# A list scheduler with fifteen fixed shifts of rank, and a third engine for one multiplication

## The chip, the cores and the metric

One NeuronCore of a Trainium2 chip. The metric is the device time of one execution in microseconds, the median of several runs of the same program.

The engines that matter here: TensorE (PE: matrix products, with PEld for its weight loads), VectorE (DVE), ScalarE (ACT), GpSimd (POOL), and SyncE (SP), which in this kernel issues nearly all DMA transfers, in order. Each engine runs its own queue in order and waits on semaphores for the others. The matrix products write to PSUM, in eight banks.

## What is computed

One post-layernorm transformer block in fp32 on x of shape (2, 512, 512), cut here to what matters:

```python
# attention: 32 query heads, 8 key/value heads (groups of 4), head width 128
q, k, v = heads(x @ Wq.T), heads(x @ Wk.T), heads(x @ Wv.T)
q, k = rmsnorm(q, q_norm_w), rmsnorm(k, k_norm_w)   # t * rsqrt(mean(t*t) + eps) * w
s = q k^T / sqrt(128) + where(rel > 0, -1e30, slope[h] * rel)
x = layernorm(x + (softmax(s) v) @ Wo.T)
# feed-forward, int32 weights with a scale per output
h = silu(gate(x)) * up(x)                           # 512 -> 1376
x = layernorm(x + down(h))                          # 1376 -> 512
```

## The kernel before, in words

**Tiles and stages.** The 1024 tokens are 8 tiles of 128 rows. Attention runs in *units*: one key/value head group g (8 of them), one batch entry b (2), one tile i of 128 queries (4), so 64 units. Two neighbouring units are a *pair* (32 pairs): its projection of 768 columns (4 query heads, one key head, one value head, each 128 wide) is made together.

For a pair, `project` (L816; the first pair has `project_plain`, L778) multiplies x by the group's weights with a scheme of seven products on half blocks (`seven`, matmuls on L674), whose sums and differences of operands (`sums_a`, `sums_b`, all recorded on L615) are made by VectorE or GpSimd. ScalarE or VectorE evicts the banks to the tile c (L771, L773), and VectorE adds others to it (L615).

`heads` (L909) then normalises the five normed heads (four query, one key) of each of the pair's two row tiles r. ScalarE squares 640 columns of c into sq (L924). VectorE sums each head to ms (L933). An epsilon is added (L947), and GpSimd raises ms to -1/2, which gives inv (L601). Then, for each r, one `tensor_tensor` multiplies c by inv, broadcast over each head's 128 columns, into sq; VectorE or GpSimd does it (L615, tiles sq<-c,inv). VectorE turns sq in blocks into c (L1069); this goes to HBM and back in another order (far_q<-c L1082, qT<-far_q L1093), and ScalarE or GpSimd weighs the key head into kT (L1107). Two (g, b) of the sixteen take their transposes from TensorE (L1026, L1041) and not from HBM.

`scores` (L1127) makes, per unit, four matmuls sc (L1144; each leaves two records in the trace), adds the bias and takes the row maxima on VectorE (L1153), the exponential on ScalarE (L1169) and the division by the row sum on ScalarE or GpSimd (L1201, L1203). `attend` (L1215) turns the attention weights: VectorE in blocks (st, L891), out to HBM (far<-st, L900) and back (prT<-far, L1264); TensorE multiplies them by v (pa, L1287; px and pz, L1319). The results aT are multiplied by Wo in an inner and outer scheme (L1511, or L674 for the last two groups) and added to acc. After the last group come layernorm (`norm1`, transposes on L1660), the feed-forward products (tiles p..._h and p..._d on L674) and the last layernorm.

**What sets the order.** Nothing is emitted when the Python code runs through these functions. `Work.add` only records an operation: a price per engine that may do it, a rank (`prio`), the function that emits it, and what it reads and writes. `Work.emit` is a greedy list scheduler: it keeps an own clock for every engine and for the DMA transfers, asks for every ready operation and every engine that may do it when it could start (inputs ready, engine free, a buffer free in the ring), and emits on each step the one that starts first; at equal starts the lower rank goes first, then the one that ends first. The instruction order of every queue, the engine of each flexible operation and the buffer of each tile come out of this.

The prices are simple lines: `pe(n) = max(0.14, n / 600)`, `act(n) = 0.15 + 0.00084 n` (0.1 more with a scale per row), `dve(n) = 0.15 + 0.00106 n`, `pool_tt(n) = 0.27 + 0.00197 n`. A transfer of m MB takes m / 0.3 us of one shared DMA clock, starts 1.6 us after its issue at the earliest, and ends 0.6 us after its share; an issue holds SP for 0.6 us. Operations marked `port` on VectorE and all of GpSimd's exclude each other in the plan.

**Ranks.** A unit u has ranks near u: its scores u, `attend` u + 0.4; a pair's projection u - 2.4 and its `heads` u - 1.8 to u - 1.4; Wqkv of a new group is loaded at u - 14, Wo at u - 10, and multiplied out near u + 2.6. The feed-forward ranks begin at 67. The start (first weights, x, the masks) has ranks from -9 to -1.

Of the kernel before, what the change touches and what calls it, by code (L numbers as in the profile page):

```python
# [2 lines left out]

# [9 lines left out]
AF = mybir.ActivationFunctionType  # L13
ALU = mybir.AluOpType
AX = mybir.AxisListType
ENG = mybir.EngineType

P = 128
B, S, DM = 2, 512, 512
H, HKV, HD = 32, 8, 128  # L20
G = H // HKV
# [37 lines left out]
def act(n, scaled=False):  # L59
    return 0.15 + 0.00084 * n + (0.1 if scaled else 0.0)  # L60


def dve(n):
    return 0.15 + 0.00106 * n


def pool_tt(n):
    return 0.27 + 0.00197 * n
# [5 lines left out]

LAG = {"PE": 0.22, "DVE": 0.1, "ACT": 0.12, "POOL": 0.2, "SP": 0.1, "ACTQ": 0.1, "NONE": 0.0}
TABLE = 1.28


class Ring:


    def __init__(self, name, bufs, shape, dtype=F32):
        self.name, self.bufs, self.shape, self.dtype = name, bufs, shape, dtype
        self.pool = None
        self.slots = [None] * bufs
        self.later = None

    def add(self, ring):

# [2 lines left out]
    def room(self, but=()):  # L92

        best = None
        if self.pool is not None:
            for k, b in enumerate(self.slots):
                if (self, k) in but:
                    continue
                t = 0.0
                for u in b.users if b else ():  # L100
                    if u["end"] is None:
                        break
                    t = max(t, u["end"] + LAG[u["eng"]])
                else:
                    if best is None or t < best[0]:
                        best = (t, self, k)
        if self.later is not None:
            found = self.later.room(but)
            if found is not None and (best is None or found[0] < best[0]):
                best = found  # L110
        return best

    def take(self, b):
        _, ring, k = self.room()
        ring.slots[k] = b
        b.tile = ring.pool.tile(
            ring.shape, ring.dtype, tag=f"{ring.name}{k}", name=b.name, bufs=1
        )


class Buf:


    def __init__(self, ring, name):
        self.ring, self.name = ring, name
        self.users = []
        self.tile = None

    def __getitem__(self, i):
        return self.tile[i]  # L130
# [2 lines left out]
class Work:  # L133


    def __init__(self):
        self.ops = []
        self.wrote, self.read = {}, {}

    def add(  # L140
        self,
        costs,
        prio,
        fn,
        reads=(),
        writes=(),
        after=(),
        table=None,
        lag=0.0,
        port=False,  # L150
        issue=0.6,
    ):


        op = {
            "issue": issue,
            "costs": costs,
            "prio": prio,
            "fn": fn,
            "deps": set(id(o) for o in after),  # L160
            "obj": list(after),
            "takes": [],
            "end": None,
            "table": table,
            "lag": lag,
            "port": port,
            "n": len(self.ops),
        }
        deps = {id(o): o for o in after}
        for key in reads:  # L170
            o = self.wrote.get(key)
            assert o is not None, (key[0].name, key[1])
            deps[id(o)] = o
        for key in writes:
            o = self.wrote.get(key)
            if o is not None:
                deps[id(o)] = o
            for o in self.read.get(key, ()):
                deps[id(o)] = o
        for key in reads:  # L180
            if key not in writes:
                self.read.setdefault(key, []).append(op)
        for key in writes:
            self.wrote[key] = op
            self.read[key] = []
        bufs = []
        for key in list(reads) + list(writes):
            b = key[0]
            if b not in bufs:
                bufs.append(b)  # L190
        for b in bufs:
            op["takes"].append(b)
            b.users.append(op)
        op["deps"] = list(deps.values())
        self.ops.append(op)
        return op

    def emit(self):
        ops = self.ops
        left = [len(o["deps"]) for o in ops]  # L200
        nexts = [[] for _ in ops]
        for o in ops:
# [6 lines left out]
        def at(o):  # L209
            t = 0.0  # L210
            for d in o["deps"]:
                t = max(t, d["end"] + d["lag"])
            return t

        for o in ops:
            if not left[o["n"]]:
                o["at"] = 0.0
                ready.append(o)
        emitted = 0
        port = {"DVE": 0.0, "POOL": 0.0}  # L220

        def room(o):

            t, but = o["at"], []
            for b in o["takes"]:
                if b.tile is not None:
                    continue
                found = b.ring.room(but)
                if found is None:
                    return None  # L230
                t = max(t, found[0])
                but.append(found[1:])
            return t

        while ready:
# [16 lines left out]
            for e, found in at_engine.items():  # L252
                first = min(found)
# [3 lines left out]
            o = ops[n]  # L257
# [14 lines left out]
                if e == "POOL" or (e == "DVE" and o["port"]):  # L272
                    port[e] = s + c
            o["start"] = s
            o["lag"] += LAG[e]
            for b in o["takes"]:
                if b.tile is None:
                    b.ring.take(b)
            o["fn"](e)
            emitted += 1  # L280
            for x in nexts[o["n"]]:
                left[x["n"]] -= 1
                if not left[x["n"]]:
                    x["at"] = at(x)
                    ready.append(x)
        assert emitted == len(ops)


@with_exitstack
def post_ln_block(  # L290
# [17 lines left out]
    nc = tc.nc  # L308
# [4 lines left out]
    W = Work()  # L313
    vec = {"DVE": nc.vector, "POOL": nc.gpsimd}
# [10 lines left out]
    rings = {}  # L325

    def ring(stage, name, bufs, shape, dtype=F32):
        r = Ring(name, bufs, shape, dtype)
        rings.setdefault(stage, []).append(r)
        return r  # L330

    def fixed(ring_, name):
# [277 lines left out]
    def tensor(n, prio, dst, a, b, alu, reads, writes, who=("DVE", "POOL"), sbuf=None, after=()):  # L610
        cost = {"DVE": dve(n), "POOL": pool_tt(n)}
        W.add(
            {e: cost[e] for e in who},
            prio,
            lambda e: vec[e].tensor_tensor(dst(), a(), b(), alu),  # L615
            reads,
            writes,
            after,
            port=len(who) > 1 if sbuf is None else sbuf,
        )  # L620
# [288 lines left out]
    def heads(p, prio):  # L909
# [7 lines left out]
        kT, v = kTs[g, b], vs[g, b]  # L917
        sq = Buf(r_sq, f"sq_{p}")
        ms, inv = Buf(r_ms, f"ms_{p}"), Buf(r_inv, f"inv_{p}")
        for r in range(2):  # L920
            W.add(
                {"ACT": act(5 * HD) + 0.05},
                prio,
                lambda e, r=r: nc.scalar.activation(  # L924
                    sq[:, r].rearrange("p h d -> p (h d)"), c(r)[:, : 5 * HD], AF.Square
                ),
                [(cb, (r, 0)), (cb, (r, 1))],
                [(sq, r)],
            )
            W.add(  # L930
                {"DVE": 0.15 + 0.135 * (G + 1)},
                prio,
                lambda e, r=r: nc.vector.tensor_reduce(ms[:, r], sq[:, r], AX.X, ALU.add),  # L933
                [(sq, r)],
                [(ms, r)],
            )


        for rs in ((0,), (1,)) if p == 0 else ((0, 1),):
# [20 lines left out]
            if p == 0:  # L960
                lead.append(W.ops[-1])
        for r in range(2):
            tensor(
                5 * HD,
                prio,
                lambda r=r: sq[:, r],
                lambda r=r: c(r)[:, : 5 * HD].rearrange("p (h d) -> p h d", h=G + 1),
                lambda r=r: inv[:, r].unsqueeze(2).to_broadcast([P, G + 1, HD]),
                ALU.mult,
                [(cb, (r, 0)), (cb, (r, 1)), (inv, r)],  # L970
                [(sq, r)],
            )


# [754 lines left out]
    def close(stage, opens, side, ends):  # L1729
        def fn(e):  # L1730
            stages[stage].close()
            for r in rings[opens]:
                r.pool = open_pool(opens, f"p_{r.name}", r.bufs, side, reuse_waits="tile")

        return W.add({"NONE": 0.0}, 0.0, fn, (), (), ends)

    def users(stage):
        seen = {}
        for o in W.ops:
            for b in o["takes"]:  # L1740
                if b.ring in rings[stage]:
                    for u in b.users:
                        seen[u["n"]] = u
        return list(seen.values())

    close("qkv", "up", "left", users("qkv"))
    close("att", "down", "right", users("att"))

    r_wi = ring("up", "wi", 1, [P, 2, NK, P], I32)
    r_wf = ring("up", "wf", 1, [P, 2, NK, P])  # L1750
# [10 lines left out]
    r_ds = ring("down", "ds", 1, [P, DM])  # L1761
    for r in (r_wi, r_wf, r_sw, r_gu):
        r.add(ring("down", r.name + "b", 1, r.shape, r.dtype))

    load(0.01, -6.0, lambda q: q.dma_start(gs_sb.tile, gs), [A(gs_sb)])
    load(0.01, -6.0, lambda q: q.dma_start(us_sb.tile, us), [A(us_sb)])
# [351 lines left out]
```

## Time and profile before

| | us |
|---|---|
| median of 3 runs | 984.5 (983.72 to 985.08) |
| the profiled execution | 983.08 |
| its span, first to last instruction | 981.3 |
| TensorE busy in it | 957.2 |
| VectorE, GpSimd, ScalarE busy | 731.4, 535.6, 451.8 |
| HBM traffic | 92.62 MB read, 53.48 MB written |

The profile is of one execution. A page sums it up: the busy time of each engine, the chain of work that ended last, the costliest groups of instructions. Groups are told apart by source line, engine, operation and the tiles they write and read (out<-in); helpers record many operations on one line, so the tiles matter more than the line. Behind a group's count stand its busy time, the mean duration of one, and the idle time of its engine just before it with what ended that. Other views give waits (who waited for whom), stretches (busy time of each engine between two times), the timeline and the chain in order of time. The clock in them is the share of TensorE's full clock that was granted. The largest single DMA groups are the attention weights' way out (112 issues of 256 KB, median 3.0 us from issue to landing) and back (224 of 128 KB, 3.1 us); a weight load of 384 KB has 5.3 us and Wo's 1024 KB 5.7 us.

### The profile page before, as it was taken

Reading aid. Unit: us, or ns where it says so; the run is one execution under the profiler, and the core shown is the slowest. Engines: PE = TensorE matmul, PEld = TensorE weight load, DVE = VectorE, ACT = ScalarE, POOL = GpSimd, SP = SyncE. Lnnn points to the kernel's source line nnn. Section 1 sums busy time; section 2 is a strip of 40 time slices with the busy share of each in tenths; the row PEclk is TensorE's granted clock in tenths of the full one; section 3 lists DMA queues with packets and bytes.
Section 4 is the critical chain, followed back from the end, with each engine's and each line's share of the span. In section 5 each row is a group of like instructions: output and inputs, shape, how many; then the busy total and the mean of one; then the engine's idle time right before and its main releaser. Section 6 shows DMA issues by size and latency. Waiting matters only on the chain.

```text
span 981.3 us, 14068 instructions
## 1 busy us (share of the span) xinstructions
PE 957.2 (98%) x4330; PEld 692.4 (71%) x4330; DVE 731.4 (75%) x1780; ACT 451.8 (46%) x1209; POOL 535.6 (55%) x582
## 2 busy tenths in 40 slices
PE   8999999999999999999999989999979999999997
PEld 5666766676767776766767666667757788888886
DVE  8777787778787788787887878797866676667544
ACT  2465364646464556456464646464445243333000
POOL 5675575868564854867386847864552322123120
PEclk9899999999999999999999999999989999999999
DMA  8123748764755765586558676656451232210001
GB/s 305 52 102 104 208 134 255 219 190 148 232 161 151 225 200 155 172 258 194 165 153 249 202 217 203 193 144 211 111 157 59 64 98 86 81 52 22 22 22 43
DMA packets 182795, 147.69 MB, mean 151 GB/s; under 512 B 26208, under 2 KB 166368, under 8 KB 181440
## 3 DMA queue, kind: packets, MB, share of 16 engines
q1 hardware_dynamic: 181856, 146.13, 48.9%
q8 instruction: 35, 0.57, 0.2%
q10 hardware_dynamic: 864, 0.66, 0.2%
q14 instruction: 40, 0.33, 0.1%
HBM read 92.62 MB, written 53.48 MB: 149 GB/s over the span
## 4 chain that ended last, share of the span: by engine, by line
PE 91%; DMA 4%; DVE 2%; SPq 1%; POOL 1%; issue 0%; ACT 0%; POOLq 0%; DVEq 0%; ACTq 0%
PE pa_q L674 15%; PE sc L1144 12%; PE pa L1287 11%; PE pa_h L674 8%; PE pb_q L674 8%; PE pa_o L1511 8%; PE pc_q L674 4%; PE pb_h L674 4%; PE pb_o L1511 4%; PE pa_d L674 4%; PE pa_o L674 3%; PE pc_o L1511 2%; DMA prT<-far 2%; PE pc_h L674 2%; PE pb_d L674 2%; PE px L1319 2%
## 5 line engine op out<-in xcount | busy, mean ns | idle before, releaser
L1169 ACT ACTIVATE pr<-pr,nmax 128x48 f32<-128x48 f32 (+15 forms) x256 | 133.5, 522 | 94.7 <-DVE nmax L1153 93.7
L1144 PE MATMUL sc<-kT,qT 128*128 128x176 f32 (+15 forms) x512 | 152.8, 411 | 2.8 <-ACT kT L1107 1.8
L1287 PE MATMUL pa<-prT,v 128*128 128x512 f32 (+1 forms) x320 | 137.4, 515 | 6.8 <-DMA prT<-far 6.8
L1153 DVE CUSTOM_DVE_ANT_0 pr<-sc,bias 128x48 f32<-128x48 f32 (+15 forms) x256 | 110.6, 442 | 43.2 <-PE sc L1144 39.6
L1144 PEld LDWEIGHTS sc<-kT,qT 128*128 128x128 f32 x512 | 88.9, 192 | 51.5 <-issue 20.3
L1201 ACT ACTIVATE pr<-pr,rden 128x64 f32<-128x64 f32 (+11 forms) x223 | 95.8, 496 | 34.0 <-DVE rden L1184 33.7
L615 DVE TENSOR_TENSOR acc<-acc,pa_o 128x512 f32<-128x512 f32 (+2 forms) x128 | 72.4, 566 | 40.3 <-PE pa_o L1511 25.0
L674 PE MATMUL pa_q<-tq,sx 128*128 128x384 f32 x248 | 90.8, 492 | 0.2 <-ACT c L771 0.2
L891 DVE STREAM_TRANSPOSE st<-pr 128x512 f32<-128x512 f32 (+1 forms) x140 | 84.0, 635 | 1.0 <-POOL si L615 0.4
L1287 PEld LDWEIGHTS pa<-prT,v 128*128 128x128 f32 x320 | 54.8, 192 | 26.8 <-issue 9.5
L771 ACT COPY c<-pa_q 128x384 f32<-128x384 f32 x79 | 37.4, 475 | 72.7 <-PE pa_q L674 71.0
L674 PEld LDWEIGHTS pa_q<-tq,sx 128*128 128x128 f32 x248 | 46.4, 192 | 31.8 <-issue 7.4
L601 POOL TENSOR_TENSOR inv<-ms,nhalf 128x10 f32<-128x10 f32 (+1 forms) x33 | 64.7, 1963 | 5.6 <-DVE ms L947 4.3
L771 ACT COPY gu<-pa_h 128x256 f32<-128x256 f32 (+1 forms) x88 | 32.0, 370 | 76.2 <-PE pa_h L674 58.2
L924 ACT ACTIVATE sq<-c 128x640 f32<-128x640 f32 x64 | 45.6, 729 | 37.1 <-DVE c L1069 27.5
L615 POOL TENSOR_TENSOR sq<-c,inv 128x640 f32<-128x640 f32 x47 | 59.5, 1276 | 0.9
L1203 POOL TENSOR_SCALAR pr<-pr,rden 128x64 f32<-128x64 f32 (+10 forms) x65 | 29.9, 469 | 53.6 <-DVE rden L1184 53.3
L771 ACT COPY aT<-pa 128x512 f32<-128x512 f32 (+1 forms) x51 | 27.4, 543 | 63.2 <-PE pa L1287 43.7
L933 DVE TENSOR_REDUCE ms<-sq 128x5 f32<-128x640 f32 x64 | 51.3, 810 | 1.3 <-ACT sq L924 1.3
L1069 DVE STREAM_TRANSPOSE c<-sq 128x320 f32<-128x320 f32 x112 | 51.0, 487 | 0.0
L1169 ACT ACTIVATION_READ_ACCUMULATOR pr<-pr,nmax 128x1 f32 x256 | 48.0, 188 | 0.0
L1511 PEld LDWEIGHTS pa_o<-ti,si 128*128 128x128 f32 x336 | 42.8, 192 | 6.9 <-issue 3.5
(237 smaller groups left out, 2202.0 us busy)
## 6 DMA issues: line engine op xcount, KB each, us to landing
far<-st SPq DMA_DIRECT2D x112, 256.0 KB, 3.0
prT<-far SPq DMA_DIRECT2D x224, 128.0 KB, 3.1
far_q<-c SPq DMA_DIRECT2D x28, 640.0 KB, 4.0
qT<-far_q SPq DMA_DIRECT2D x56, 320.0 KB, 3.8
w<-in_wqkv_dram SPq DMA_DIRECT2D x39, 384.0 KB, 5.3
wo<-in_wot_dram SPq DMA_DIRECT2D x10, 1024.0 KB, 5.7
far<-st SPq DMA_DIRECT2D x28, 128.0 KB, 2.3
prT<-far SPq DMA_DIRECT2D x56, 64.0 KB, 3.0
```

Source lines behind the costliest of these rows:

```text
L601: lambda e: nc.gpsimd.tensor_tensor(dst(), src(), nhalf[:, :n], ALU.pow),
L615: lambda e: vec[e].tensor_tensor(dst(), a(), b(), alu),
L674: nc.tensor.matmul(bank[:rows, :width], lhsT=a(fa, c), rhs=b(fb, c), start=(fresh and c == 0), stop=(c == depth - 1), skip_group_check=True,)
L771: nc.scalar.copy(dst(), src())
L891: {"DVE": dve(n)}, prio, lambda e: nc.vector.transpose(dst(), src()), reads, [A(st)]
L933: lambda e, r=r: nc.vector.tensor_reduce(ms[:, r], sq[:, r], AX.X, ALU.add),
L1144: lambda e, a=a, w=w, sc=sc: nc.tensor.matmul(sc[:, :w], lhsT=qT[:, r, a, : G * Q], rhs=kT[:, :w], start=True, stop=True),
L1153: lambda e, a=a, w=w, sc=sc: nc.vector.tensor_tensor_reduce(out=pr[:, a, :w], in0=sc[:, :w], in1=bias[:, S - w :], scale=-(SHRINK**-g), sc ...
L1169: lambda e, a=a, w=w: nc.scalar.activation(pr[:, a, :w], pr[:, a, :w], AF.Exp, bias=nmax[:, a : a + 1], scale=-1.0, accum_out=den[:, a : a ...
L1201: nc.scalar.activation(dst, src, AF.Copy, scale=rden[:, a : a + 1])
L1287: lambda e, j=j, prT=prT, n=n: nc.tensor.matmul(by_head(po.tile)[:, :, P - n // G :], lhsT=v[:, j, :], rhs=late(prT, j, n), start=(j == 0) ...
L1511: nc.tensor.matmul(bank[:, ts(c, P)], lhsT=a(fa, c), rhs=b(fb, c), start=fresh and c == 0, stop=True, skip_group_check=True,)
```

## The change

The scheduler is split. `Work.order` makes the plan and emits nothing: rings are reset, a buffer gets a place (`home`) and not yet a tile, and a pool counts as open from the planned step that opens it (`opens`). `Work.emit` first calls `shift` once for each of fifteen seeds, then makes one plan and emits it in that order. A shift draws a centre, a reach and a scale; every operation whose first rank lies within the reach of the centre has its rank moved by a normal deviate of that scale, the same one for all operations of equal first rank and equal engines. The moves of several shifts add up. The seeds stand in the code as constants: by the words that came with the change, a shift was kept for the time that the plan reckons itself.

The multiplication of the heads by their norm is recorded with three engines in place of two. On ScalarE it is five ACTIVATEs, one per head, each a copy of 128 columns with a scale per row. VectorE's price for it rises by 0.2 us, so that the plan has 1.03 (VectorE), 1.53 (GpSimd) and 1.79 us (ScalarE). A second variant, squares with their sums on ScalarE, is written but is chosen by `ALONE`, which is false for every pair. A lag that was added to an operation on emission is now added where it is read, with the same value.

```diff
+SHIFTS = (
+    1000003, 1000006, 1000008, 1000014, 1000017, 1000025, 1000044, 1000058, 1000062, 1000075,
+    1000109, 1000133, 1000283, 1000470, 1000520,
+)
+NORMED = {"DVE": dve(5 * HD) + 0.2, "POOL": pool_tt(5 * HD), "ACT": 5 * act(HD, True)}
+WHO = ("DVE", "POOL", "ACT")
+ALONE = lambda p, r: False
...
+    def shift(self, seed):
+
+        rnd = random.Random(seed)
+        at, reach, by = rnd.uniform(-9, 100), rnd.choice((1, 3, 8, 30)), rnd.choice((0.1, 0.3, 1.0))
+        moved = {}
+        for o in self.ops:
+            if abs(o["first"] - at) < reach:
+                key = o["first"], tuple(sorted(o["costs"]))
+                if key not in moved:
+                    moved[key] = rnd.gauss(0, by)
+                o["prio"] += moved[key]
+
+    def emit(self):
+        for seed in SHIFTS:
+            self.shift(seed)
+        for o in self.order():
+            for b in o["takes"]:
+                if b.tile is None:
+                    b.make()
+            o["fn"](o["eng"])
...
         for r in range(2):
-            tensor(
-                5 * HD,
+
+            def normed(e, r=r):
+                if e == "ACT":
+                    for h in range(G + 1):
+                        nc.scalar.activation(
+                            sq[:, r, h, :],
+                            c(r)[:, ts(h, HD)],
+                            AF.Copy,
+                            scale=inv[:, r, h : h + 1],
+                        )
+                    return
+                vec[e].tensor_tensor(
+                    sq[:, r],
+                    c(r)[:, : 5 * HD].rearrange("p (h d) -> p h d", h=G + 1),
+                    inv[:, r].unsqueeze(2).to_broadcast([P, G + 1, HD]),
+                    ALU.mult,
+                )
+
+            W.add(
+                {k: NORMED[k] for k in WHO},
                 prio,
-                lambda r=r: sq[:, r],
-                lambda r=r: c(r)[:, : 5 * HD].rearrange("p (h d) -> p h d", h=G + 1),
-                lambda r=r: inv[:, r].unsqueeze(2).to_broadcast([P, G + 1, HD]),
-                ALU.mult,
+                normed,
                 [(cb, (r, 0)), (cb, (r, 1)), (inv, r)],
                 [(sq, r)],
+                port=True,
             )
```

## The prediction, made before the change had run

> **What bounds the kernel now.** I read the page first: the engines' shares, then the chain that ended last.
>
> ```profile
> span 981.3 us, 14068 instructions
> ...
> PE 957.2 (98%) x4330; PEld 692.4 (71%) x4330; DVE 731.4 (75%) x1780; ACT 451.8 (46%) x1209; POOL 535.6 (55%) x582
> ...
> PE 91%; DMA 4%; DVE 2%; SPq 1%; POOL 1%; issue 0%; ACT 0%; POOLq 0%; DVEq 0%; ACTq 0%
> ```
>
> TensorE is busy 957.2 of 981.3 us and is 91% of the chain. The change alters no matmul, so only TensorE's idle time can go: 981.3 - 957.2 = 24.1 us. The view of waits, for TensorE alone, says what ended it:
>
> ```profile
> engine line waited for: us in total, times, longest us
> PE pa L1287 <- DMA prT<-far: 6.8, 5, 3.0
> PE ptq L1026 <- DVE sq L615: 2.8, 1, 2.8
> PE sc L1144 <- ACT kT L1107: 1.8, 1, 1.8
> PE warm L481 <- POOL ident masks.py:199: 1.3, 1, 1.3
> PE pa_h L674 <- ACT gu L771: 1.1, 1, 1.1
> PE sc L1144 <- DVE nmax L1153: 0.9, 2, 0.6
> PE ptx L1660 <- DVE acc L1633: 0.9, 1, 0.9
> ```
>
> The whole list comes to 17.6 us; the rest is 6.3 us behind the last matmul, which ends at 975.0 in the timeline (972.70 + 2.32). The greatest item is the attention weights' way through HBM (far, then prT). Where this lies is shown by the sums over stretches (us, TensorE, weight loads, DVE, ACT, POOL, clock, DMA share, GB/s):
>
> ```profile
> 20.00:40.00 20.00, 17.36 (x60) 11.16 (x61) 14.27 (x32) 6.99 (x20) 13.22 (x13) 0.83 0.40 147
> 140.00:170.00 30.00, 27.75 (x131) 18.86 (x130) 23.72 (x64) 17.96 (x52) 20.51 (x21) 1.00 0.82 243
> 480.00:500.00 20.00, 18.91 (x102) 13.50 (x100) 15.76 (x34) 7.04 (x18) 11.25 (x10) 1.00 0.69 212
> 555.00:575.00 20.00, 17.53 (x59) 9.84 (x58) 15.80 (x39) 11.53 (x32) 14.09 (x14) 1.00 0.92 272
> 700.00:735.00 35.00, 29.65 (x127) 20.65 (x126) 25.06 (x73) 14.94 (x41) 18.35 (x23) 0.90 0.45 135
> 760.00:770.00 10.00, 8.94 (x40) 6.22 (x39) 4.99 (x11) 3.74 (x6) 1.33 (x2) 1.00 0.19 52
> ```
>
> First number less second is idle TensorE: 2.25 us at 140, 1.09 at 480, 2.47 at 555, 5.35 at 700, 1.06 at 760. The first 40 us hold 5.3. At 555 the DMA engines are 92% busy: the timeline has four weight loads issued at 556.14 and the spill of the attention weights at 558.65, and the chain lets that spill land 6.42 us later, where the page's median is 3.0. At 700 the clock too is under 1. The timeline and a narrower stretch say why:
>
> ```profile
> 719.89 2.05 PE L1287 MATMUL pa<-prT,v 128*128 128x512 f32 x2 [3.02 <-DMA prT<-far]
> ```
> ```profile
> 712.00:720.00 8.00, 3.20 (x18) 1.96 (x16) 5.98 (x21) 5.48 (x19) 4.65 (x4) 0.76 0.85 289
> 719.00:724.00 5.00, 4.11 (x9) 2.34 (x10) 4.04 (x7) 0.00 (x0) 2.48 (x3) 0.60 0.63 174
> ```
>
> TensorE ran 3.20 of 8 us and then waited 3.02 us, and afterwards ran at a lowered clock: (1 - 0.60) x 5.00 = 2.0 us of clock missing. It was idle for the first 0.89 us of that stretch, where half a clock (0.45 us) costs nothing, so about 1.55 us were lost in work. That hole cost 4.6 us in all.
>
> **The shifts.** Each seed draws a centre, a reach and a scale. Drawn out, the fifteen centres (reach) are 47.2 (8), 28.4 (3), 92.0 (30), 52.7 (30), 47.8 (30), 52.8 (8), 18.9 (3), 63.7 (1), 81.4 (30), 52.5 (3), 63.4 (3), 69.6 (1), 84.3 (1), 21.3 (1), 72.3 (1); scales are 0.1 to 1.0 rank. No rank below 15.9 is moved. Ranks count units, and every unit has 8 score matmul records: there are 96 by 153 us (unit 12), 334 by 489 (unit 41.8), 384 by 566 (unit 48), 484 by 713 (unit 60.5). So the holes at 480, 555 and 700 lie inside the reaches; the one at 760 starts the feed-forward ranks (67 on), reached by 69.6 and 92.0; the holes at the start and at 163 lie below them all.
>
> Does the plan see the holes that the chip has? Its prices against rows: ACT copy of 384 columns 0.473 us, row 0.475; DVE 0.557, row 0.552; POOL power 1.97, row 1.963; a 0.4 MB weight load 1.33 us of DMA time, so four take 5.3, and the spill behind them is late in the plan as in the trace. It doesn't price the lowered clock. So a plan that is shorter should be shorter on the chip for the DMA holes, in part.
>
> Terms: reachable holes 1.09 + 2.47 + 5.35 + 1.06 + 1.55 (clock) = 11.5 us. Ends: all of it goes (-11.5), or new holes of the same total open (+11.5), since every queue's order after rank 16 is redrawn, SP's with it, and a transfer that lands late there holds all issues behind it. I take half, -5.8: the plan's prices fit the rows on the engines, but a greedy order that closes one hole tends to open a smaller one. SP issues no more DMAs than before; what is late next is the following unit's spill.
>
> **The start and 140 to 170.** Ranks there are unmoved; only the new engine choice reaches them. Ends: -2.8 (the wait for sq at 21 us goes) to +2.8 (it doubles); I take 0, since there VectorE, free, already multiplies in 0.83 us.
>
> **The norm on ScalarE.** The multiplication sq<-c,inv runs 64 times now:
>
> ```profile
> L615 POOL TENSOR_TENSOR sq<-c,inv 128x640 f32<-128x640 f32 x47 | 59.5, 1276 | 0.9
> ...
> L615 DVE TENSOR_TENSOR sq<-c,inv 128x640 f32<-128x640 f32 x17 | 14.3, 846 | 1.6 <-POOL inv L601 1.6
> ```
> ```profile
> L1201 ACT ACTIVATE pr<-pr,rden 128x128 f32<-128x128 f32 x9 | 3.5, 388 | 0.0
> ```
>
> On ScalarE it is five ACTIVATEs of 128 columns with a scale per row: at most 5 x 0.388 = 1.94 us; at least 5 x 0.29 = 1.45, since the timeline has four smaller ones of that line in 1.16 us. I take 1.7. The planner picks the engine that can start first, and at equal starts the cheaper end, so ScalarE gets the second of a pair when POOL has the first and VectorE is busy: I guess 20 of 64. That adds 20 x 1.7 = 34 us to ScalarE (46% to 50%) and takes 20 x 1.28 = 26 us from POOL (55% to 52%). Neither bounds. Queued behind such a norm are evictions of projection banks (ACT c) and exponentials. Ends: -1.8 (the wait of sc for kT, the end of the chain that the norm begins, goes) to +7.8 (TensorE waits for ACT in four rows, kT, gu, aT and c; each longer by a norm of 1.94). I take 0: TensorE's own queue hides it as long as a bank is free; uncovered, one costs up to 1.94 us. The 0.2 us that the plan adds to VectorE's price, and the flag that is false throughout, cost nothing on the chip.
>
> A page speaks against this part: the Trainium skill, "ScalarE: Activation LUTs", Rules for kernel authors, has products go to VectorE rather than ScalarE. The trace agrees on duration: 0.846 us on VectorE against at least 1.45. Priced by the rule, with every moved norm on the path, it would add 20 x (1.7 - 0.85) = 17 us; the waits above show no such path, so I do not.
>
> **The sum.** Profiled execution: 983.08 us, span 981.3 and 1.78 around it. 981.3 - 5.8 + 0 + 0 = 975.5; + 1.78 = 977.3. The median shown is 984.5, 1.42 above this execution, so 978.7 is forecast.
>
> **Rivals.**
> *A longer hole (slower).* Place: the way far to prT behind a bulk load on SP, ranks over 16. A redrawn order leaves a spill behind four weight loads or the 1 MB output weights just as TensorE has no other work. Price as at 719: 3.0 + 1.6 = 4.6 us each, over the forecast. One new one gives 978.7 + 4.6 = 983.3, no change; from two it decides: 987.9; three 992.5. For it: DMA share 0.92 at 555 and 0.82 at 140; the plan doesn't price the clock. Against: 224 + 56 such transfers, and only 5 stalled TensorE.
>
> *The holes only move.* The plan's gain is in waits that the chip doesn't have; the sum of holes stays: 984.5. For it: spills land between 2.3 and 6.4 us where the plan has one price. ScalarE's rival gives about the same: 978.7 + 7.8 = 986.5, if the norms stand ahead of evictions in four places. Against: ScalarE idles 71 us before copies of c until TensorE is done.
>
> *All reachable holes go*, and the kT wait: 984.5 - 11.5 - 1.8 = 971.2. For it: several shifts lie on each hole. Against: the transposes of the last norms at 713 hang on a chain of DVE and POOL, which no order shortens.
>
> The Trainium skill, "TensorE: Matmul & The Clock Gate", Part 1, has the clock halve after an idle window of about 3.4 us. The row at 712 to 720 agrees in kind, with a single wait of 3.02 us in a stretch 40% busy. By the rule alone a hole of 3.0 us keeps the clock, and the slower rival's two holes would give 978.7 + 6.0 = 984.7, no change.
>
> **How the numbers follow.** Forecast, 976 to 982: 0.48; all holes go, below 976: 0.10; so faster by over 0.2% (under 982.5, about what a measurement can tell) 0.58. Holes move, ScalarE, or one new hole (982.5 to 986.5): 0.15. Two or more new holes: 0.27. The range of 970 to 990 takes the bound of 971.2 and half of the slower rival; out of it are about 0.04 below and 0.13 above.
>
> **What would show it.** Right: span near 975.5; TensorE idle 16 to 20 us with its busy time within 3 us of 957; the wait of pa for prT below 6.8; 700 to 735 with a clock of 1; the start's 2.8 us wait unchanged; an ACT group sq<-c,inv of some 100 instructions. Wrong: a new hole of about 3 us with a clock under 1 behind it; waits of TensorE for ACT of over 5 us; TensorE's busy time changed by more than 3 us; or no ACT group at all, which leaves the shifts alone.

## The result, and the profile after

The changed kernel takes **971.0 us** (median of 4 runs, 970.48 to 973.81) against 984.27 for the kernel before (4 runs): ratio 0.987, 95% interval 0.985 to 0.989. It is faster, by 13.3 us where 5.8 were forecast. The profiled execution is the slowest of the four, 973.81 us with a span of 972.0; in an experiment below the same kernel was profiled again, with a span of 966.5.

The page of the changed kernel, the lines that answer to those shown of before:

```profile
span 972.0 us, 14179 instructions
...
PE 955.3 (98%) x4330; PEld 692.5 (71%) x4330; DVE 716.8 (74%) x1765; ACT 487.5 (50%) x1342; POOL 531.6 (55%) x592
...
PE 95%; DMA 3%; DVE 1%; SPq 0%; POOL 0%; issue 0%; POOLq 0%; DVEq 0%
```

TensorE's idle time fell from 24.1 to 972.0 - 955.3 = 16.7 us, so 7.4 of the span's 9.3 us; 1.9 are in its busy time. TensorE has 95% of the chain in place of 91%. Its waits in the same view:

```profile
PE pa_o L725 <- DMA wo<-in_wot_dram: 4.9, 2, 2.5
PE ptq L1109 <- ACT sq L1034: 2.8, 1, 2.8
PE warm L532 <- POOL ident masks.py:199: 1.3, 1, 1.3
PE pa_o L1594 <- DVE acc L666: 0.8, 2, 0.6
PE pb_q L725 <- DVE xT L666: 0.5, 1, 0.5
PE pa L1370 <- DMA prT<-far: 0.4, 2, 0.2
```

The wait for prT, 6.8 us before, is down to 0.4, and those for kT, gu and the layernorm's acc are gone. The wait at the start is the same 2.8 us. One wait of some size is new: for the output weights (wo), twice, 4.9 us together. The same stretches as before (us, TensorE, weight loads, DVE, ACT, POOL, clock, DMA share, GB/s) have no idle time left:

```profile
140.00:170.00 30.00, 30.00 (x134) 19.92 (x133) 23.48 (x55) 17.34 (x49) 18.93 (x18) 1.00 0.76 244
480.00:500.00 20.00, 20.00 (x116) 15.10 (x115) 14.37 (x27) 7.38 (x19) 16.05 (x14) 1.00 0.68 220
555.00:575.00 20.00, 20.00 (x81) 12.94 (x80) 16.88 (x47) 12.84 (x37) 13.65 (x13) 1.00 0.69 195
700.00:735.00 35.00, 35.00 (x164) 26.78 (x163) 25.83 (x78) 18.27 (x52) 18.47 (x25) 0.97 0.39 121
760.00:770.00 10.00, 10.00 (x48) 8.81 (x47) 7.10 (x17) 1.12 (x3) 3.93 (x6) 1.00 0.01 2
```

TensorE is busy all the time in each; before it idled 2.25 + 1.09 + 2.47 + 5.35 + 1.06 = 12.2 us there. The two executions are not always at the same work at the same time. By 153 us both have 96 score matmul records behind them, by 489 they have 334 and 336; but the 484 of the greatest hole of before, at 713, are here reached by 693:

```profile
0.00:693.00 693.00, 144.00 (x484) 82.15 (x484) 1.00 0.61 187
```

So the place of that hole has to be looked for some 20 us earlier, and there a hole is left. The two new holes, from the timeline, and a stretch around the second:

```profile
664.97 1.10 PE L725 MATMUL pa_o<-wo,aT 128*128 128x256 f32 x4 [2.40 <-DMA wo<-in_wot_dram]
695.60 2.08 PE L725 MATMUL pa_o<-wo,aT 128*128 128x256 f32 x4 [2.51 <-DMA wo<-in_wot_dram]
```
```profile
695.00:702.00 7.00, 6.40 (x16) 5.12 (x17) 2.22 (x5) 0.34 (x3) 5.06 (x4) 0.51 0.53 160
```

The last number but two is the clock: 0.51 behind the second hole, where the same four matmuls take 2.08 us, against 1.10 behind the first. The transfer was issued at 687.15 and TensorE could go on at 695.60, some 8.4 us; the plan prices it at 1.6 + 3.5 + 0.6 = 5.7. In the repeated run this wait is 1.3 us, one time, and no half clock follows it.

The multiplications by the norm:

```profile
L1034 ACT ACTIVATE sq<-c,inv 128x128 f32<-128x128 f32 x160 | 50.1, 389 | 14.6 <-POOL inv L652 14.6
L1041 POOL TENSOR_TENSOR sq<-c,inv 128x640 f32<-128x640 f32 x23 | 29.0, 1263 | 0.9
L1041 DVE TENSOR_TENSOR sq<-c,inv 128x640 f32<-128x640 f32 x9 | 10.2, 1139 | 4.4 <-POOL inv L652 4.4
```

160 ACTIVATEs are 32 of the 64 multiplications, and 50.1 / 32 = 1.57 us is one.

### The profile page after: what moved, and what is told of

Read it like the earlier page. It is cut to its first block, busy times and chain, and to the rows that moved or that the text cites. A ratio compares the mean times of both kernels' runs of the same rounds, so it can differ in the third digit from the quotient of the medians.

```text
span 972.0 us, 14179 instructions
## 1 busy us (share of the span) xinstructions
PE 955.3 (98%) x4330; PEld 692.5 (71%) x4330; DVE 716.8 (74%) x1765; ACT 487.5 (50%) x1342; POOL 531.6 (55%) x592
## 4 chain that ended last, share of the span: by engine, by line
PE 95%; DMA 3%; DVE 1%; SPq 0%; POOL 0%; issue 0%; POOLq 0%; DVEq 0%
PE pa_q L725 16%; PE sc L1227 12%; PE pa L1370 11%; PE pb_q L725 8%; PE pa_h L725 8%; PE pa_o L1594 8%; PE pb_h L725 4%; PE pb_o L1594 4%; PE pc_q L725 4%; PE pa_d L725 4%; PE pa_o L725 3%; PE pc_h L725 2%; PE pc_o L1594 2%; PE pb_d L725 2%; DMA wo<-in_wot_dram 2%; PE px L1402 2%
## 5 line engine op out<-in xcount | busy, mean ns | idle before, releaser
L1227 PE MATMUL sc<-kT,qT 128*128 128x48 f32 (+15 forms) x512 | 153.3, 408 | 0.0
L1227 PEld LDWEIGHTS sc<-kT,qT 128*128 128x128 f32 x512 | 86.9, 191 | 42.1 <-issue 19.2
L1284 ACT ACTIVATE pr<-pr,rden 128x64 f32<-128x64 f32 (+12 forms) x213 | 92.3, 495 | 16.1 <-DVE rden L1267 15.9
L652 POOL TENSOR_TENSOR inv<-ms,nhalf 128x10 f32<-128x10 f32 (+1 forms) x33 | 65.7, 1992 | 22.1 <-DVE ms L1014 20.8
L977 ACT ACTIVATE sq<-c 128x640 f32<-128x640 f32 x64 | 45.2, 730 | 32.0 <-DVE c L1152 23.4
L1034 ACT ACTIVATE sq<-c,inv 128x128 f32<-128x128 f32 x160 | 50.1, 389 | 14.6 <-POOL inv L652 14.6
L1286 POOL TENSOR_SCALAR pr<-pr,rden 128x64 f32<-128x64 f32 (+10 forms) x75 | 34.8, 475 | 37.4 <-DVE rden L1267 37.2
L666 POOL TENSOR_TENSOR si<-so 128x384 f32<-128x384 f32 x21 | 21.0, 1001 | 59.1 <-PE pb_o L1594 57.1
```

What stands on the lines that cost most here:

```text
L652: lambda e: nc.gpsimd.tensor_tensor(dst(), src(), nhalf[:, :n], ALU.pow),
L1227: lambda e, a=a, w=w, sc=sc: nc.tensor.matmul(sc[:, :w], lhsT=qT[:, r, a, : G * Q], rhs=kT[:, :w], start=True, stop=True),
L1284: nc.scalar.activation(dst, src, AF.Copy, scale=rden[:, a : a + 1])
```

## The experiments

Two questions. Is the gain the order, the third engine, or both? And what does the plan's own time, by which the shifts were kept, say of the chip? The scheduler is Python in the kernel, so its plan can be made without emitting anything; its time is the latest end in it. It is 960.9 us for the kernel before and 948.0 for the changed one: 12.9 less in the plan, 13.3 less on the chip. (That these two agree so closely is luck, as the table below shows.)

Three theories. *Plan* (later *order*): the chip follows the plan's time, with about 23 us on top. *Additive*, the prediction's: each part has its price, the norm's is nothing. *Relief*, the rival: ScalarE takes work from GpSimd and VectorE, and that is the gain.

**The third engine alone.**

```diff
-SHIFTS = (1000003, ... 1000520)
+SHIFTS = ()
```

> The third engine for the norm, and its 0.2 us on VectorE's price, without any shift. Plan theory (the chip follows the time that the plan reckons, which is 960.9 us for the kernel before and 970.0 for this one, and the chip takes 984.3 - 960.9 = 23.4 more): 993.4 us, slower than before. Additive theory (the prediction's terms: the norm on ScalarE costs and gains nothing by itself): 984.3, no change. Relief theory (ScalarE takes 32 multiplications from GpSimd and VectorE, and that is the gain): near 971 to 976.

Measured: 988.68 us, ratio 1.0065 (1.0042 to 1.0088), slower. The plan's 970.0 has a hole of 8.5 us on TensorE before 549.0. The chip has it, in its own time, 11.6 us on:

```profile
560.59 1.12 PE L1224 MATMUL sc<-kT,qT 128*128 128x48 f32 x4 [7.24 <-ACT kT L1187]
```

Additive and relief theory both fail here, and the plan shows where; its time, with 23.4 us on top, is 4.7 us too long.

**The shifts alone.**

```diff
-NORMED = {"DVE": dve(5 * HD) + 0.2, ...
-WHO = ("DVE", "POOL", "ACT")
+NORMED = {"DVE": dve(5 * HD), ...
+WHO = ("DVE", "POOL")
```

> The fifteen shifts, with the norm on VectorE or GpSimd at the old prices. Plan theory (plan 985.7): 1009 us, about 2.5% slower than before. Additive theory: the shifts hold the gain, so 971. Relief theory: about 984, no change.

Measured: 1011.53 us, ratio 1.0288 (1.0259 to 1.0318). Either part alone makes the kernel slower; together they make it faster. The plan (985.7) has its longest hole, 7.2 us, before 559.8; the chip again has one of 5.17 us there, 12.5 us on:

```profile
572.34 0.66 PE L1227 MATMUL sc<-kT,qT 128*128 128x48 f32 x2 [5.17 <-ACT kT L1190]
```

**The price alone.** As the shifts alone, but without shifts and with the 0.2 us kept in VectorE's price.

```diff
-SHIFTS = (1000003, ... 1000520)
-WHO = ("DVE", "POOL", "ACT")
+SHIFTS = ()
+WHO = ("DVE", "POOL")
```

> Nothing but 0.2 us added to VectorE's price in the plan for one multiplication (64 of them); no shift, no third engine. Plan theory (plan 994.1): 1017 us, 3.4% slower. Additive and relief theory: a price in the plan costs nothing on the chip, 984.3, no change.

Measured: 1022.3 us, ratio 1.0398 (1.0368 to 1.0428). No engine does anything new; one number in the plan moved, and the order that came out costs 39 us. TensorE's greatest waits there:

```profile
PE pa L1367 <- DMA prT<-far: 13.9, 9, 3.5
PE pa_o L1591 <- DVE acc L663: 12.8, 8, 5.3
```

**Five shifts of the fifteen.**

```diff
-        for seed in SHIFTS:
+        for seed in SHIFTS[:5]:
```

> The whole change with the first five of the fifteen shifts. Plan theory (plan 955.8): 979 us. Additive theory: the holes that the later shifts lie on (52.8, 63.7, 52.5, 63.4) stay, 700 to 735 among them, so 977 to 980. Relief theory: 971 to 973, as the third engine is there in full.

Measured: 977.92 us, ratio 0.9935 (0.9912 to 0.9957). The plan theory said 979, the additive one 977 to 980: this run doesn't tell them apart. It excludes the relief theory's 971 to 973.

**The same order, the norm back on GpSimd.**

```diff
-            o["fn"](o["eng"])
+            o["fn"]("POOL" if "norm" in o and o["eng"] == "ACT" else o["eng"])
...
+            W.ops[-1]["norm"] = r
```

> The changed kernel's order of instructions kept as it is, but the 32 multiplications that its plan gave to ScalarE are emitted on GpSimd at the same places. Plan theory (the plan's clocks run over this fixed order with those engines give 981.6 us, against 948.0): 1004. Additive theory (the norm's engine is off the path, an error of at most 7.8 us): 971 to 979. Relief theory (the third engine is the gain by itself): about 984, the time before.

Measured: 970.46 us, ratio 0.9863 (0.9815 to 0.9911), the changed kernel's time, without ScalarE in the multiplication:

```profile
L1041 POOL TENSOR_TENSOR sq<-c,inv 128x640 f32<-128x640 f32 x55 | 71.3, 1313 | 1.3
L1041 DVE TENSOR_TENSOR sq<-c,inv 128x640 f32<-128x640 f32 x9 | 12.2, 1361 | 4.4 <-POOL inv L652 4.4
```

In this order the engine is worth nothing on the chip; the additive theory holds for it. One wait grew, at the start, where TensorE waits 4.7 us for sq in place of 2.8, and others shrank by as much. The plan theory, stretched to an order that the plan hadn't made, is wrong by 34 us.

**The order of before, the norm on ScalarE.** The kernel before by its order, prices and two engines; only the second of each pair is emitted elsewhere.

```diff
-            o["fn"](o["eng"])
+            o["fn"]("ACT" if o.get("norm") == 1 else o["eng"])
...
+            W.ops[-1]["norm"] = r
```

> The order of the kernel before kept as it is, but the second of each pair's two multiplications (32 of 64, 12 of VectorE's and 20 of GpSimd's) is emitted on ScalarE at the same place. Plan theory (the plan's clocks over this fixed order: 972.0 against 960.9): 995. Additive theory: 982 to 992, with 984 the likeliest. Relief theory: 971 to 976.

Measured: 982.97 us beside 982.98 for the kernel before, ratio 0.9995 (0.9975 to 1.0015): no change. TensorE's waits are nearly those of before (the one for prT is 5.0 in place of 6.8), though 32 multiplications moved:

```profile
PE pa L1368 <- DMA prT<-far: 5.0, 5, 3.0
PE ptq L1107 <- DVE sq L1038: 2.7, 1, 2.7
PE sc L1225 <- ACT kT L1188: 1.8, 1, 1.8
PE warm L529 <- POOL ident masks.py:199: 1.3, 1, 1.3
PE pa_h L722 <- ACT gu L819: 1.1, 1, 1.1
```

The relief theory has fallen, and the plan theory shrinks to an order theory: the order carries the time.

**Shifts that nobody chose.**

```diff
-SHIFTS = (1000003, ... 1000520)
+SHIFTS = tuple(range(3600, 3615))
```

> The third engine, and fifteen shifts whose seeds nobody chose (3600 to 3614) in place of the fifteen kept ones. Plan theory (plan 978.2, which is also the median of 34 such sets): 1001. Theory that any stirring of the ranks closes half the holes, since the order before was stuck with them: 975 to 980.

Measured: 992.97 us, ratio 1.0101 (1.0078 to 1.0124): slower, though 8 us below what the plan theory said. Stirring the ranks is not what helps; of 60 such sets of fifteen, 26 have no plan at all (no operation can start at some step), and the 34 others reach from 955.6 to 1027.0 in the plan.

**A search without the third engine.** The prices and engines of before, and shifts kept by a search of its own.

```diff
-SHIFTS = (1000003, ... 1000520)
-NORMED = {"DVE": dve(5 * HD) + 0.2, ...
-WHO = ("DVE", "POOL", "ACT")
+SHIFTS = (12, 20, 129, 157, 193, 237, 599, 1355)
+NORMED = {"DVE": dve(5 * HD), ...
+WHO = ("DVE", "POOL")
```

> The kernel before with its two engines for the norm and its prices, and eight shifts of its own, kept by a search of 1500 seeds. Plan 951.4. Order theory: 974 to 975, so that nearly all of the gain comes without the third engine. Rival (the third engine is what lets an order gain): 981 to 985.

Measured: 970.35 us, ratio 0.9856 (0.9826 to 0.9887). The changed kernel itself, run beside it:

> The changed kernel unaltered, for its time on the same chip as the three others: 971 by its first runs; all theories agree.

Measured: 969.71 us, ratio 0.985 (0.9819 to 0.988). Eight shifts and two engines give the whole gain, and the time is 4 us under the 974 to 975 that the plan's 951.4 stood for. The profile of this repeat, and two of its waits:

```profile
span 966.5 us, 14179 instructions
...
PE 952.1 (99%) x4330; PEld 691.2 (72%) x4330; DVE 716.8 (74%) x1765; ACT 487.0 (50%) x1342; POOL 531.3 (55%) x592
```
```profile
PE pa L1370 <- DMA prT<-far: 2.0, 2, 1.8
PE pa_o L725 <- DMA wo<-in_wot_dram: 1.3, 1, 1.3
```

**The output weights in four transfers.** Aimed at the wait for wo. The third engine stays, and the shifts are sixteen of a search of its own.

```diff
-SHIFTS = (1000003, ... 1000520)
+SHIFTS = (1, 20, ... 1143)
...
-        load(1.05, prio, lambda q: q.dma_start(wo.tile, wot[g]), [(wo, m) for m in range(4)])
+        for m in range(4):
+            load(0.2625, prio + 0.001 * m, lambda q, m=m: q.dma_start(wo[:, m], wot[g, :, m]), [(wo, m)])
```

> A version meant to beat both: the third engine kept, the output weights of a group loaded as four transfers of 256 KB in place of one of 1024 KB, and a search of its own over 1500 seeds, which kept 16. Plan 943.6 us. Order theory (an order that the plan made costs the plan's time and some 23 us on the chip): 967, and TensorE's waits for the output weights (4.9 us in the changed kernel's trace) gone. Rival (the plan has reached what it can see and holes that it can't see fill the rest): 971, as the changed kernel.

Measured: 968.25 us, ratio 0.984 (0.9807 to 0.9873). The wait for wo is gone, but one for prT is back (3.3 us), and its runs (967.2 to 971.27) overlap those of the changed kernel beside it (968.27 to 971.12): not told apart.

**The same, with a dearer price.** 0.375 in place of 0.2625, and a search of its own, which kept twenty shifts.

> As the version with four transfers of the output weights, but each priced in the plan by 1.25 us in place of 0.875, nearer to what the traces show, and with its own search, which kept 20 shifts. Plan 945.9. Order theory: 969; if the dearer price keeps holes away that the cheaper one leaves, 966 or less, and below the version with the cheaper price.

Measured: **964.57 us** (963.92 to 965.48), ratio 0.9799 (0.9764 to 0.9834), the fastest of all; its slowest run is under the fastest of the changed kernel beside it (968.27).

```profile
span 962.6 us, 14253 instructions
...
PE 949.0 (99%) x4330; PEld 689.5 (72%) x4330; DVE 715.0 (74%) x1764; ACT 485.7 (50%) x1335; POOL 528.2 (55%) x600
```

A price and a search changed at once here, so what the price itself gave stays open.

All orders that the plan made, side by side:

| order | plan us | chip us | chip less plan |
|---|---|---|---|
| price alone | 994.1 | 1022.3 | 28.2 |
| shifts alone | 985.7 | 1011.5 | 25.8 |
| unchosen shifts | 978.2 | 993.0 | 14.8 |
| third engine alone | 970.0 | 988.7 | 18.7 |
| before | 960.9 | 984.3 | 23.4 |
| five shifts | 955.8 | 977.9 | 22.1 |
| search without ScalarE | 951.4 | 970.4 | 19.0 |
| the change | 948.0 | 971.0 | 23.0 |
| wo in four, dearer | 945.9 | 964.6 | 18.7 |
| wo in four | 943.6 | 968.3 | 24.7 |

The rows come from several sets of runs, beside which the kernel before took 983.0 to 986.0 us, so differences of 3 us between rows of different sets say little. Over 50 us the plan ranks the orders as the chip does, though chip less plan runs from 14.8 to 28.2. Over the last 8 it no longer ranks them: chip less plan scatters by 6 us among them.

## Why the prediction was right and wrong

**Right: the bound and the place.** TensorE's idle time was what could go, and the four stretches named are full in the first profile; in the repeat 1.78 us are idle between 700 and 735. The wait of pa for prT went from 6.8 to 0.4 us (2.0 in the repeat), and the 2.8 us at the start stayed (2.5).

**Wrong: the size of the sum.** The step that failed is "I take half, -5.8", with 0 for all else. By parts, from the span of the profile before (us):

| | forecast | first profile | repeat |
|---|---|---|---|
| four stretches, less the new holes | -5.0 | -5.1 | -6.9 |
| 140 to 170 | 0 | -2.2 | -2.2 |
| rest of TensorE's idle time | 0 | -0.1 | -0.6 |
| TensorE's busy time (the clock) | -0.8 | -1.9 | -5.1 |
| span | -5.8 | -9.3 | -14.8 |

The four stretches lost all of their 1.09 + 2.47 + 5.35 + 1.06 = 9.97 us; new waits, 4.9 us for wo in the first profile, 1.3 for wo and 1.8 for prT in the repeat, stand against them. So the reason given for the half, that a greedy order closing one hole opens a smaller one, holds in these traces: at unit 60.5, where 5.35 us were lost, 2.5 are still lost in the first profile, with a half clock behind them. Mis-sized were the terms beside it, the clock and 140 to 170; the median's 13.3 us lies between the two profiles.

The clock was looked for behind one hole, at 1.55 us, and then halved. Over the whole trace of before the mean clock was 0.992, so that 0.008 x 981.3 = 7.9 us of it were missing. In the changed kernel it was 0.994 (5.8 us missing), in the repeat 0.998 (1.9), in the fastest kernel 1.000. TensorE's busy time, 957.2 before, was 955.3, 952.1 and 949.0, with the same 4330 records: it fell by 1.9, 5.1 and 8.2 us where the missing clock fell by some 2, 6 and 8. So a hole can cost twice, as idle time and as a lower clock behind it, and the second part hides in the busy time. The sign "its busy time within 3 us of 957" was right in the first profile and wrong in the repeat.

An estimate of the total was to be had from the plan, which nets holes closed against holes opened: without a shift its time is 970.0, with five 955.8, with fifteen 948.0. (Made anew after each seed, nine of the fifteen shorten it, two lengthen it by less than half a us, and the last four leave it.) The prediction compared three of the plan's prices with rows, found them right within 1% (it left out GpSimd's multiplication, 1.53 us against a row of 1.276), and drew from it "in part"; it gives no time of the plan.

**Wrong: the stretch from 140 to 170.** It was held to be out of reach, since no rank there is moved, and put at 0. Its 2.25 us went. An order is made step by step; a different engine for one operation reorders all that follows, and needs no rank to do it. The run of the third engine alone, without any shift, shows it:

```profile
140.00:170.00 30.00, 30.00 (x132) 19.81 (x131) 23.51 (x56) 17.35 (x47) 18.95 (x18) 1.00 0.78 246
```

**Wrong: "The 0.2 us ... cost nothing on the chip".** Alone they cost 39 us, through the order. The same mistake lies under the whole sum: parts were priced one by one and added. The measured parts are +0.65% for the third engine with its price, +2.9% for the shifts and -1.3% for both.

**Misread: the hole at 555.** The spill that landed after 6.42 us is one of 128 KB, whose row on the page has 2.3 us and not 3.0. And most of the hole was no wait for the weights that it carried: 1.81 of the 2.47 us were the wait for kT.

```profile
far<-st SPq DMA_DIRECT2D x28, 128.0 KB, 2.3
```
```profile
569.52 0.66 PE L1144 MATMUL sc<-kT,qT 128*128 128x48 f32 x4 [1.81 <-ACT kT L1107]
```

**Right: the norm on ScalarE is worth 0**, in both directions (the norm moved back: 970.46; moved in place: 0.9995). The guess of 20 was 32, and 1.7 us was 1.57. GpSimd did not go down to 52% but stayed at 55%: with 24 multiplications fewer it ran 592 instructions in place of 582, as the new order gave it other work.

**Rivals.** A longer hole came, but the transfer that was late was a bulk load itself and not a spill behind one: 4.9 us in two waits, and a clock of 0.51 behind the second. The plan's price, 5.7 us, was short there of the 8.4. This is the prediction's own sign of being wrong, and the kernel was faster all the same. That the holes only move is refuted: TensorE's idle time went from 24.1 to 16.7 us, and to 14.4 in the repeat. "All reachable holes go", at 971.2, had the time, with a chance of 0.10, but by luck: it knew of no new hole, left out 140 to 170 and most of the clock, and counted the wait for kT twice, as it lies within the 2.47 us at 555.

## What to carry to other kernels

Where a planner writes the order, a change to a price, an engine or a rank is not the sum of its parts: predict it by the plan as a whole, after seeing that its prices fit the rows and its holes lie where the trace has them. A plan kept for its own time keeps its gain on the chip as far as it ranks the orders as the chip does; here it did over 50 us and no longer over the last 8. To know whether an engine or an order brings a gain, emit the same order with the other engine.

## What the runs showed of the hardware

The clock records of the traces show the half clock in pieces of 3.41, 6.83 and 10.24 us, in all of these kernels but the fastest, which has it only at its very end. All changes of a trace lie on one grid of 3.413 us: in the changed kernel the half clock begins at 22.56 and at 694.98 us, 197.0 such steps apart. A single wait of 2.51 us was followed by one (at 695) and one of 2.40 us was not (at 665). The grid cut the two waits differently. The first left TensorE 1.52 us of work in the step before the change; the second fell into two steps, with 1.72 and 2.71 us of work:

```profile
691.57:694.98 3.41, 1.52 (x8) 0.98 (x6) 1.76 (x7) 3.00 (x8) 1.39 (x2) 1.00 0.27 70
```
```profile
660.85:664.26 3.41, 1.72 (x7) 0.81 (x5) 1.79 (x5) 1.76 (x5) 0.00 (x1) 1.00 0.89 310
664.26:667.68 3.42, 2.71 (x13) 2.43 (x14) 1.48 (x3) 0.00 (x0) 2.71 (x3) 1.00 0.11 32
```

The Trainium skill, "TensorE: Matmul & The Clock Gate", Part 1, has a free-running window of 3.413 us; the grid agrees with it. No step ahead of these two changes was idle as a whole, and the work in a step doesn't settle it alone: in the kernel before, a step with 1.61 us of work (from 159.85) was followed by no change, and one with 1.96 us (from 712.81) was. What decides stays open.

The plan never lets GpSimd run beside an operation of VectorE that is marked `port`. In the run with the norm back on GpSimd, records of the two do overlap, but a multiplication and another such operation on SBUF tiles don't get on side by side. Seven of GpSimd's 55 multiplications began while VectorE ran an operation with two inputs in SBUF; they took 1.34 to 1.90 us, and each ended 1.11 to 1.12 us after VectorE's. The 48 others took 1.25 to 1.27 us. The five of VectorE's nine that began behind one of GpSimd's all ended 0.68 us after it. So the second waits for the first, and the wait stands in its record. A pair of each order, and a third that is not like them:

```profile
74.39 0.83 DVE L1041 TENSOR_TENSOR sq<-c,inv 128x640 f32<-128x640 f32 x1 [1.86 <-POOL inv L652]
74.43 1.90 POOL L1041 TENSOR_TENSOR sq<-c,inv 128x640 f32<-128x640 f32 x1
```
```profile
540.63 1.25 POOL L1041 TENSOR_TENSOR sq<-c,inv 128x640 f32<-128x640 f32 x1
541.12 1.58 DVE L666 TENSOR_TENSOR tq<-w,tq 128x768 f32<-128x768 f32 x1
```
```profile
379.38 1.99 POOL L652 TENSOR_TENSOR inv<-ms,nhalf 128x10 f32<-128x10 f32 x1
379.92 0.68 DVE L666 TENSOR_TENSOR wo<-wo 128x512 f32<-128x512 f32 x1
```

VectorE's operation in the last pair lies wholly inside GpSimd's power and takes its usual 0.68 us. So the plan is right to keep the multiplications apart, and too strict with the power. With the exclusion lifted altogether and GpSimd's price for the multiplication at 1.26 us in place of 1.53, the plan's clocks give 951.8 in place of 981.6 us for that fixed order, nearer to the 970.46 less some 20 that the chip took. This is worked out, not tried, and lifts more than the traces allow: which operations a plan should keep apart stays open.
